# Cross-attention over 64 sequences: another order of loads in the first rounds, and two normalisings in the tail moved to ScalarE and GpSimd

## The chip, the core and the metric

The kernel runs on one core of a Trainium2 chip. The metric is the device time of one execution in microseconds; of several runs the median is given. The engines of the core are named as the profile names them: PE (TensorE, with PEld for its weight loads), DVE (VectorE), ACT (ScalarE), POOL (GpSimd) and SP (SyncE, which only issues DMAs here).

## What is computed

`x` is 64 x 256 x 512, `ctx` is 64 x 256 x 384, all in float32. Each of the 64 sequences goes through one cross-attention layer of hidden size 512:

```python
text_p  = einsum('bld,dh->blh', x,   W_text)  + b_text
audio_p = einsum('bsd,dh->bsh', ctx, W_audio) + b_audio
Q = layer_norm(text_p, g1, beta1)
K = layer_norm(audio_p, g2, beta2)
V = audio_p
alpha = softmax(einsum('blh,bsh->bls', Q, K) / sqrt(512), axis=-1)
H = einsum('bls,bsh->blh', alpha, V)
H = einsum('blh,hk->blk', H, W_out) + b_out
out = layer_norm(H + x, g_out, beta_out)
```

`layer_norm` takes mean and variance over the last axis, with an epsilon of 1e-5.

## The kernel before

**Staging.** The work is software-pipelined over rounds, one per sequence b, in an order written out by hand (each engine runs its instructions in the order in which the program names them). In round b the kernel computes the scores and the softmax of sequence b (`at`), the projection to Q and to K of sequence b+2 (`q2`, `k2`), the context product and output product of sequence b-1 (`last`), and the residual, the final layer norm and the store of sequence b-2 (`done`). Rounds run for b = 0 to 61; before them stands a start-up for sequences 0 and 1 and the folding of the weights, and behind them a written-out tail for sequences 62 (`at`) and 63 (`end`), in which `last` and `done` are sequences 61 and 60.

**Products.** The projections and the output product use a block scheme with seven products instead of eight (`Blocks.products` on PE, `Blocks.leave` for the evictions on DVE, line 483); each takes sums of blocks that POOL prepares (`sum_x`, `sum_c`). Their PSUM tiles are the pool `p_pj` of six banks; a bank is free again when both of its products have left. The scores are on line 511, the context product `ps_z` on line 577. W_audio and W_out are folded into one matrix at the start.

**Turning.** PE needs its operands with the contracted axis on the partitions. Outside the tail, the turning goes through DRAM and DVE: normalised Q and K rows and the exponentials are stored to DRAM (`qd`, `kd`, `ed`) and read back by four DMAs each, in squares (`squares`, line 88: `qq`, `kq`, `eq`), and DVE transposes 32x32 blocks (`turn`, line 91, and line 439). `x` and `ctx` are read the same way straight from the inputs (`xq`, `cq`; `load_x`, `load_c`) and turned by `turn_next(b + 3)`, which also makes the sums on POOL. The row-wise copies of `x` (for the residual, `add_x` on POOL, line 593) and of `ctx` (for the context product) are loaded by `load_rows` into pools of three buffers each.

**The DMA queue.** All these DMAs are issued by SP in program order, and an issue waits until its source is written. In a round of before the order is: `qq` and `kq` of b+1 (four each), `ed` of b, `cq` and `xq` of b+4 (four each), `eq` of b (four), the rows of x and of ctx of b+1, the output of b-2, `qd` and `kd` of b+2. `go_sb` and `beo_sb`, the scale and the shift of the last layer norm broadcast over the partitions, are loaded by two DMAs ahead of round 0.

**DVE in a round.** The order in a round from round 1 on: the last evictions of `done`, the turning of the exponentials of b-1 (`last.turn_e`, tile `eT`), of x and ctx of b+3 (`xT`, `cT`), the maxima of the scores (`nmx`), the evictions of `q2`, `q[b+1].turn`, the two `shift`s of `done`, `k[b+1].turn`, the two `settle`s of `done`, the evictions of `k2` and of `last`'s output. In round 0 `k[1].turn` and `turn_next(3)` stand at other places.

**The tail's last layer norms.** For each of the row tiles 0 and 1 of sequences 62 and 63: `evict` (line 632: PSUM times 1/denominator plus x, then mean and variance; `evict_halves` for the last one, lines 672 to 681), `scales` (POOL: variance plus epsilon, line 341; power of -0.5, line 343; the tiles `ve` and `rstd`), `shift` (DVE, line 698: minus the mean, times `go`), `settle` (DVE, line 703: times `rstd`, plus `beo`; `settle_halves`, line 686, for the last one), and the store.

Of the kernel before, what the change touches and what calls it, by code (L numbers as in the profile page):

```python
# [9 lines left out]
F32 = mybir.dt.float32  # L10
AF = mybir.ActivationFunctionType
ALU = mybir.AluOpType
# [3 lines left out]
P = 128  # L16
SQ = 32
NQ = P // SQ
EPS = 1e-05
# [3 lines left out]
def kernel(  # L23
# [41 lines left out]
    nc = tc.nc  # L65
    ctx.enter_context(tc.manual_schedule())
    B, L, D = x.shape
    S, DA = c.shape[1:]
    H = w_text.shape[1]
    LT, ST = L // P, S // P  # L70
    DC, AC, HC = D // P, DA // P, H // P
    scale = 1.0 / math.sqrt(H)

    const = ctx.enter_context(tc.tile_pool(name="const", bufs=1))
    xin = ctx.enter_context(tc.tile_pool(name="xin", bufs=3))
    cin = ctx.enter_context(tc.tile_pool(name="cin", bufs=3))
    blk = ctx.enter_context(tc.tile_pool(name="blk", bufs=2))
    work = ctx.enter_context(tc.tile_pool(name="work", bufs=2))
    small = ctx.enter_context(tc.tile_pool(name="small", bufs=4))
# [16 lines left out]
    def load_c(b):  # L96
        cq = blk.tile([P, S // SQ, DA // NQ], F32, tag="cq", name=f"cq_{b}")
        squares(cq, c[b])
        blocks[b] = [cq]

    def load_x(b):
        xq = blk.tile([P, L // SQ, D // NQ], F32, tag="xq", name=f"xq_{b}")
        squares(xq, x[b])
        blocks[b].append(xq)

    def load_squares(b):
        load_c(b)
        load_x(b)

    def load_rows(b):  # L110
        x_sb = xin.tile([P, LT, D], F32, tag="x", name=f"x_{b}")
        c_sb = cin.tile([P, ST, DA], F32, tag="c", name=f"c_{b}")
        nc.sync.dma_start(x_sb, x[b].rearrange("(t p) d -> p t d", p=P))
        nc.sync.dma_start(c_sb, c[b].rearrange("(t p) d -> p t d", p=P))
        return x_sb, c_sb

    ident = const.tile([P, P], F32, tag="ident", name="ident")
    make_identity(nc, ident)
    nhalf = const.tile([P, 2], F32, tag="nhalf", name="nhalf")
# [12 lines left out]
    def row(v, name):  # L132
        t = const.tile([P, H], F32, tag=name, name=name)
        nc.sync.dma_start(t, v.rearrange("(o h) -> o h", o=1).broadcast_to([P, H]))
        return t
# [4 lines left out]

    x_0 = xin.tile([P, LT, D], F32, tag="x", name="x_0")
    c_0 = cin.tile([P, ST, DA], F32, tag="c", name="c_0")
    c_rows, x_rows = [v[0].rearrange("(t p) d -> p t d", p=P) for v in (c, x)]
    wa_sb = const.tile([P, AC, H], F32, tag="wa", name="wa")
    wt_sb = const.tile([P, DC, H], F32, tag="wt", name="wt")

# [2 lines left out]
        for q in range(NQ):  # L149
            queues[q].dma_start(t[q * SQ : (q + 1) * SQ, lo : lo + n], v[q, :, lo : lo + n])  # L150

    nc.sync.dma_start(c_0[:, :1], c_rows[:, :1])
    weight_chunks(wa_sb, w_audio, 0, 1, [nc.scalar, nc.sync, nc.scalar, nc.sync])
    weight_chunks(wa_sb, w_audio, 1, 2, [nc.sync] * NQ)
    nc.sync.dma_start(c_0[:, 1:], c_rows[:, 1:])
    for t in range(LT):
        nc.sync.dma_start(x_0[:, t, :], x_rows[:, t, :])
    weight_chunks(wt_sb, w_text, 0, 2, [nc.sync] * NQ)
    ba_sb = row(b_audio, "ba")
    weight_chunks(wt_sb, w_text, 2, 2, [nc.sync] * NQ)  # L160
# [123 lines left out]
    H2 = H // 2  # L284
# [50 lines left out]
    def rstd_of(var, n, total=False):  # L335

        ve = small.tile([P, n], F32, tag="ve", name="ve")
        if total:
            nc.gpsimd.tensor_scalar(ve, var, 1.0 / D, EPS, ALU.mult, ALU.add)
        else:  # L340
            nc.gpsimd.tensor_scalar(ve, var, EPS, None, ALU.add)  # L341
        r = small.tile([P, n], F32, tag="rstd", name="rstd")
        nc.gpsimd.tensor_tensor(r, ve, nhalf[:, :n], ALU.pow)  # L343
        return [r[:, t : t + 1] for t in range(n)]
# [154 lines left out]
    class Attention:  # L499
        def __init__(self, b):  # L500
            self.b, self.qT, self.kT = b, q.pop(b).T, k.pop(b).T
            self.xb, self.c_sb = rows[b]

        def scores(self, end=False):
            if end:
# [84 lines left out]

        def add_x(self):
            for t in range(LT):
                nc.gpsimd.tensor_tensor(self.y[:, t, :], self.y[:, t, :], self.xb[:, t, :], ALU.add)  # L593

        def statistics(self):

# [34 lines left out]
        def evict(self, t):  # L631
            nc.vector.scalar_tensor_tensor(  # L632
                self.y[:, t, :],
                self.ps_y.pop(t),
                self.rden[:, t : t + 1],
                self.xb[:, t, :],
                ALU.mult,
                ALU.add,
            )
            moments(self.mv, self.y[:, t, :], t)  # L640

        def scales(self, lo=0, n=LT):
            self.r = getattr(self, "r", {})
            self.r.update({lo + t: r for t, r in enumerate(rstd_of(self.mv[:, lo : lo + n, 1], n))})

        def moments(self, tiles=range(LT)):
            if 0 in tiles:
# [20 lines left out]
        def evict_halves(self, t):  # L668
            st = small.tile([P, 2, 6], F32, tag="st2", name="st2")
            for h in range(2):  # L670
                half = self.y[:, t, bass.ts(h, H2)]
                nc.vector.scalar_tensor_tensor(
                    half,
                    self.ps_h[h],
                    self.rden[:, t : t + 1],
                    self.xb[:, t, bass.ts(h, H2)],
                    ALU.mult,
                    ALU.add,
                )
                nc.vector.bn_stats(st[:, h, :], half)  # L680
            nc.vector.bn_aggr(self.mv[:, t, :], st)
# [46 lines left out]
    def turn_next(b):  # L728
        xT[b] = turn_x(b)
        xs[b] = sum_x(xT.pop(b))  # L730
        cT[b] = turn_c(b)
        cs[b] = sum_c(cT.pop(b))

    def add_bias(b):
        xb = rows[b][0]
        for t in range(LT):
            nc.gpsimd.tensor_tensor(xb[:, t, :], xb[:, t, :], bao_sb, ALU.add)

    assert B > 3
    q, k, xT, cT, rows = {}, {}, {}, {}, {0: (x_0, c_0)}  # L740


    c_turn = RowTurn(c_0, AC, "cT")
# [105 lines left out]
    q[1].normalise()  # L849
    q[1].store()  # L850
    q[1].fetch()
    go_sb = row(g_out, "go")
    beo_sb = row(beta_out, "beo")

    done = last = None
    for b in range(B - 2):
        three = b + 3 < B
        at = Attention(b)
        at.scores()
        if done:  # L860
            done.o.leave(3)
            done.o.leave(7)
            done.o.leave(4)
            done.add_x()
        if last:
            last.turn_e()
        if three and b:
            turn_next(b + 3)
        at.maxima()
        at.exponentials()  # L870
        if not b:
            k[1].turn()
        q2 = q[b + 2] = Blocks("q", b + 2, xs.pop(b + 2), wt_blocks, bt_sb)
        q2.products(1, 2)
        q2.leave(1)
        at.reciprocals()
        at.divide_e()
        if not b:
            k[1].affine(g2_sb, be2_sb)
        if b:  # L880
            q[b + 1].fetch()
            k[b + 1].fetch()
        at.store_e()
        if b + 4 < B:
            load_squares(b + 4)
        at.fetch_e()
        rows[b + 1] = load_rows(b + 1)
        if done:
            done.statistics()
        q2.products(6, 5)  # L890
        q2.leave(6)
        q2.leave(2)
        q2.leave(5)
        q2.products(7, 3)
        q2.leave(3)
        q2.leave(7)
        q2.products(4)
        q2.leave(4)
        q2.square()
        q2.scales()  # L900
        q[b + 1].turn()
        if not b:
            turn_next(3)
        if done:
            done.shift(0)
            done.shift(1)
        if last:
            last.context()
        q[b + 1].affine(g1_sb, be1_sb)
        if b:  # L910
            k[b + 1].turn()
            k[b + 1].affine(g2_sb, be2_sb)
        if done:
            done.settle(0)
            done.settle(1)
            done.store()
        q2.normalise()
        q2.store()
        if last:
            last.start_products()  # L920
        k2 = k[b + 2] = Blocks("k", b + 2, cs.pop(b + 2), wa_blocks, ba_sb)
        k2.products(1, 2)
        k2.leave(1)
        k2.products(6, 5)
        k2.leave(6)
        k2.leave(2)
        k2.leave(5)
        k2.products(7, 3)
        k2.leave(3)
        k2.leave(7)  # L930
        k2.products(4)
        k2.leave(4)
        k2.square()
        k2.scales()
        k2.normalise()
        k2.store()
        if last:
            last.o.products(1, 2)
            last.o.leave(1)
            last.o.products(6, 5)  # L940
            last.o.leave(6)
            last.o.leave(2)
            last.o.leave(5)
            last.o.products(7, 3)
            last.o.products(4)
        done, last = last, at


    at = Attention(B - 2)
    q[B - 1].fetch()  # L950
    k[B - 1].fetch()
    rows[B - 1] = load_rows(B - 1)
    at.scores()
    done.o.leave(3)
    done.o.leave(7)
# [53 lines left out]
    at.multiply(1)  # L1009
    at.shift(0)  # L1010
    at.evict(1)
    at.scales(1, 1)
    at.settle(0)
    end.context()
    end.start_output()
    end.multiply(0)
    at.shift(1)
    at.settle(1)
    at.store()
    end.evict(0)  # L1020
    end.scales(0, 1)
    end.multiply_halves(1)
    end.shift(0)
    end.evict_halves(1)
    end.scales(1, 1)
    end.shift(1)
    end.settle(0)
    end.store(0, 1)
    end.settle_halves(1)

# [31 lines left out]
```

## Time and profile before

| | us |
|---|---|
| median of 3 runs | 1419.27 |
| lowest, highest of the runs | 1417.74, 1419.90 |
| the profiled execution | 1418.87 |
| its span in the profile | 1417.1 |
| mean time of a 128x256 scores matmul | 0.379 |
| shift or settle of a 128x512 row tile in the tail, DVE | 0.74 to 0.75 |
| addition on a 128x512 row tile, POOL (line 593) | 1.278 |
| ACT scaling a 128x512 row tile: scale alone; scale and bias | 0.714; 0.806 |
| `rstd` of one row tile, POOL | 0.56 to 0.93 |

The profile is of one execution; its span runs from the first to the last record, and the execution's time has 1.8 us more. "Busy" of an engine leaves out DMA issues and waits. Timelines give the start in us from the start of the span, the length, engine, line, operation, output and inputs, and in square brackets how long the engine was idle before and what ended that. The page puts 96% of the chain of work that ended last on PE.

### The profile page before, as it was taken

How to read it: one execution, taken by the hardware profiler on the slowest of the kernel's cores; microseconds unless marked ns; L12 is line 12 of the kernel's file. 1: busy time of each engine (PE TensorE's matmuls, PEld its weight loads, DVE VectorE, ACT ScalarE, POOL GpSimd, SP SyncE). 2: the span in 40 equal slices, each digit the busy share in tenths (PEclk: the TensorE clock that was granted, in tenths of full speed). 3: DMA queues.
4: the chain of work that ended last, by engine and by line, in shares of the span. 5: the costliest groups of instructions: out<-in, count | busy, mean ns of one | idle time of the engine just before them, and what ended most of it. 6: DMA issues, size and time to landing. Idle time of an engine off the chain costs nothing.

```text
span 1417.1 us, 23332 instructions
## 1 busy us (share of the span) xinstructions
PE 1404.4 (99%) x6441; PEld 1220.4 (86%) x6441; DVE 1273.0 (90%) x2134; ACT 931.8 (66%) x2293; POOL 878.0 (62%) x1295
## 2 busy tenths in 40 slices
PE   9999999999999999999999999999999999999997
PEld 5888888888888888888888888888888888888885
DVE  5789999999998999999999999999999999999988
ACT  4666676676676676765766766767667667667662
POOL 4556656666666666575566666665765666666645
PEclk9999999999999999999999999999999999999999
DMA  8898887888887788888878878887888788788763
GB/s 203 227 244 238 240 243 214 238 240 221 235 234 232 227 224 244 237 223 235 243 216 238 240 216 239 231 235 228 228 239 239 220 238 240 218 238 233 220 191 118
DMA packets 450583, 322.61 MB, mean 228 GB/s; under 512 B 154901, under 2 KB 382997, under 8 KB 450453
## 3 DMA queue, kind: packets, MB, share of 16 engines
q1 hardware_dynamic: 450356, 320.98, 79.9%
q8 instruction: 53, 0.87, 0.3%
q14 instruction: 78, 0.63, 0.2%
q10 hardware_dynamic: 96, 0.13, 0.0%
HBM read 204.09 MB, written 116.92 MB: 227 GB/s over the span
## 4 chain that ended last, share of the span: by engine, by line
PE 96%; DMA 1%; POOL 1%; DVE 1%; SPq 0%; issue 0%; ACT 0%; POOLq 0%; DVEq 0%; ACTq 0%
PE ps_q L472 27%; PE ps_y L472 21%; PE ps_k L472 21%; PE ps_sc L511 16%; PE ps_z L577 11%; DMA wt<-in_L_xattn_W_text_dram 1%; DMA xq<-in_x_dram 1%; POOL rstd L343 0%; PE ps_wao L245 0%; DVE st L267 0%; SPq L150 0%; POOL ve L341 0%; DVE y L632 0%; DVE y L698 0%; POOL wtsum L293 0%
## 5 line engine op out<-in xcount | busy, mean ns | idle before, releaser
L341 POOL TENSOR_SCALAR ve<-var 128x2 f32<-128x2 f32 x126 | 44.5, 353 | 305.9 <-ACT junk L380 305.9
L511 PE MATMUL ps_sc<-kT,qT 128*128 128x256 f32 x1024 | 231.5, 379 | 0.0
L528 ACT ACTIVATE e<-ps_sc,nmx 128x256 f32<-128x256 f32 x128 | 59.5, 469 | 246.4 <-DVE nmx L521 246.4
L483 DVE TENSOR_TENSOR qr<-ps_q,qr 128x512 f32<-128x512 f32 x378 | 188.0, 511 | 35.7 <-PE ps_q L472 24.0
L511 PEld LDWEIGHTS ps_sc<-kT,qT 128*128 128x128 f32 x1024 | 194.6, 190 | 26.9 <-ACT qT L446 0.2
L483 DVE TENSOR_TENSOR kr<-ps_k,kr 128x512 f32<-128x512 f32 x378 | 188.1, 511 | 24.3 <-PE ps_y L472 0.5
L483 DVE TENSOR_TENSOR yr<-ps_y,yr 128x512 f32<-128x512 f32 x372 | 185.1, 511 | 23.4
L593 POOL TENSOR_TENSOR yr<-yr,x 128x512 f32<-128x512 f32 x124 | 157.2, 1278 | 57.1 <-DVE yr L483 57.0
L577 PE MATMUL ps_z<-eT,c 128*128 128x256 f32 x768 | 176.5, 379 | 0.1
L472 PE MATMUL ps_q<-wtsum,xsum 128*128 128x256 f32 x756 | 173.6, 379 | 0.6 <-POOL xsum L305 0.6
L343 POOL TENSOR_TENSOR rstd<-ve,nhalf 128x2 f32<-128x2 f32 (+1 forms) x194 | 159.3, 821 | 16.2
L472 PE MATMUL ps_k<-wa,cT 128*128 128x256 f32 x630 | 166.8, 379 | 0.0
L472 PE MATMUL ps_y<-wao,zT 128*128 128x256 f32 x620 | 164.2, 379 | 0.0
L577 PEld LDWEIGHTS ps_z<-eT,c 128*128 128x128 f32 x768 | 145.8, 190 | 20.7 <-ACT e L528 0.5
L472 PEld LDWEIGHTS ps_q<-wtsum,xsum 128*128 128x128 f32 x756 | 143.6, 190 | 20.5 <-POOL xsum L305 1.0
L380 ACT ACTIVATE junk<-kr 128x512 f32<-128x512 f32 x126 | 79.3, 630 | 98.9 <-DVE kr L483 98.9
L446 ACT ACTIVATE qT<-qT,columns 128x256 f32<-128x256 f32 x256 | 132.8, 592 | 6.6 <-DVE qT L91 6.6
L472 PEld LDWEIGHTS ps_k<-wa,cT 128*128 128x128 f32 x630 | 119.6, 190 | 16.2
L446 ACT ACTIVATE kT<-kT,columns 128x256 f32<-128x256 f32 x256 | 132.1, 588 | 1.1 <-DVE kT L91 1.0
L472 PEld LDWEIGHTS ps_y<-wao,zT 128*128 128x128 f32 x620 | 117.7, 190 | 16.0
L408 ACT ACTIVATE kr<-kr,rstd 128x512 f32<-128x512 f32 x126 | 84.1, 714 | 70.7 <-POOL rstd L343 70.7
L703 DVE SCALAR_TENSOR_TENSOR yr<-yr,rstd,beo 128x512 f32<-128x512 f32 x124 | 127.5, 1066 | 0.6 <-POOL rstd L343 0.6
(150 smaller groups left out, 2945.9 us busy)
## 6 DMA issues: line engine op xcount, KB each, us to landing
kd<-kr SPq DMA_DIRECT2D x64, 512.0 KB, 3.1
kq<-kd SPq DMA_DIRECT2D x256, 128.0 KB, 3.4
qd<-qr SPq DMA_DIRECT2D x64, 512.0 KB, 5.5
qq<-qd SPq DMA_DIRECT2D x256, 128.0 KB, 3.3
xq<-in_x_dram SPq DMA_DIRECT2D x252, 128.0 KB, 2.9
x<-in_x_dram SPq DMA_DIRECT2D x63, 512.0 KB, 4.1
out_dram<-yr SPq DMA_DIRECT2D x62, 512.0 KB, 5.0
cq<-in_ctx_dram SPq DMA_DIRECT2D x252, 96.0 KB, 2.5
```

Source lines behind the costliest of these rows:

```text
L341: nc.gpsimd.tensor_scalar(ve, var, EPS, None, ALU.add)
L343: nc.gpsimd.tensor_tensor(r, ve, nhalf[:, :n], ALU.pow)
L380: nc.scalar.activation(junk, self.rows[:, t, :], AF.Square, scale=1.0 / math.sqrt(H), accum_out=self.var[:, t : t + 1],)
L408: nc.scalar.mul(row, row, self.r[t])
L446: nc.scalar.activation(self.T[:, k, :], self.T[:, k, :], AF.Identity, bias=bet[:, k : k + 1], scale=gam[:, k : k + 1],)
L472: nc.tensor.matmul(bank[:, j, :], lhsT=side, rhs=w, start=(i == 0), stop=(i == len(pairs) - 1))
L483: add = lambda o, i0, i1: nc.vector.tensor_tensor(o, i0, i1, ALU.add)
L511: nc.tensor.matmul(self.sc[:, t, :], lhsT=self.qT[:, k, bass.ts(t, P)], rhs=self.kT[:, k, :], start=(k == 0), stop=(k == HC - 1),)
L528: nc.scalar.activation(self.e[:, t, :], self.sc[:, t, :], AF.Exp, bias=self.nmx[:, t : t + 1], accum_out=self.den[:, t : t + 1],)
L577: nc.tensor.matmul(ps[:, j, :], lhsT=self.c_sb[:, s, bass.ts(lo + j, P)], rhs=self.eT[:, s, :], start=(s == 0), stop=(s == ST - 1),)
L593: nc.gpsimd.tensor_tensor(self.y[:, t, :], self.y[:, t, :], self.xb[:, t, :], ALU.add)
L703: nc.vector.scalar_tensor_tensor(self.y[:, t, :], self.y[:, t, :], self.r[t], beo_sb, ALU.mult, ALU.add)
```

## The change

In the rounds:

- The rows of x and of ctx are loaded by two functions, and the rows of x of sequence b in round b instead of round b-1 (round 61 loads those of 61 and 62; those of sequence 63 and all rows of ctx stay where they were).
- In round 0, `eq` is read ahead of `xq` instead of behind it.
- `go_sb` and `beo_sb` are loaded at the end of round 0, behind `kd` of sequence 2.
- From round 1 to 60, DVE turns x and ctx of b+3 before the exponentials of b-1.

In the tail:

- `scale_soon` puts the addition of epsilon on DVE and leaves the power on POOL, for row 1 of sequence 62 and both rows of 63.
- Row 1 of sequence 62 is settled by ACT (times `rstd`) and POOL (plus `beo`).
- Row 0 of sequence 63 is normalised by ACT (times `rstd`, minus mean times `rstd`) and POOL (times `go`, plus `beo`), in place of `shift` and `settle` on DVE.

The order of PE's instructions is the same. The diff, without renamings:

```diff
-    def load_rows(b):
-        x_sb = xin.tile([P, LT, D], F32, tag="x", name=f"x_{b}")
-        c_sb = cin.tile([P, ST, DA], F32, tag="c", name=f"c_{b}")
-        nc.sync.dma_start(x_sb, x[b].rearrange("(t p) d -> p t d", p=P))
-        nc.sync.dma_start(c_sb, c[b].rearrange("(t p) d -> p t d", p=P))
-        return x_sb, c_sb
+    def load_x_rows(b):
+        x_rows[b] = xin.tile([P, LT, D], F32, tag="x", name=f"x_{b}")
+        nc.sync.dma_start(x_rows[b], x[b].rearrange("(t p) d -> p t d", p=P))
+
+    def load_c_rows(b):
+        c_rows[b] = cin.tile([P, ST, DA], F32, tag="c", name=f"c_{b}")
+        nc.sync.dma_start(c_rows[b], c[b].rearrange("(t p) d -> p t d", p=P))
...
+        def scale_soon(self, t, shift=False):
+
+            r = small.tile([P, 1], F32, tag="rone", name="rone")
+            ve = small.tile([P, 1], F32, tag="veone", name="veone")
+            nc.vector.tensor_scalar(ve, self.mv[:, t, 1:2], EPS, None, ALU.add)
+            nc.gpsimd.tensor_tensor(r, ve, nhalf[:, :1], ALU.pow)
+            self.r = getattr(self, "r", {})
+            self.r[t] = r
+            if shift:
+                self.nmr = small.tile([P, 1], F32, tag="nmrone", name="nmrone")
+                nc.gpsimd.tensor_scalar(
+                    self.nmr, self.mv[:, t, 0:1], r, -1.0, ALU.mult, ALU.mult
+                )
+
+        def settle_beside(self, t):
+
+            row = self.y[:, t, :]
+            nc.scalar.mul(row, row, self.r[t])
+            nc.gpsimd.tensor_tensor(row, row, beo_sb, ALU.add)
+
+        def finish_beside(self, t):
+
+            row = self.y[:, t, :]
+            nc.scalar.activation(row, row, AF.Identity, bias=self.nmr, scale=self.r[t])
+            nc.gpsimd.tensor_tensor(row, row, go_sb, ALU.mult)
+            nc.gpsimd.tensor_tensor(row, row, beo_sb, ALU.add)
...
     q[1].fetch()
-    go_sb = row(g_out, "go")
-    beo_sb = row(beta_out, "beo")
...
             done.add_x()
+        if three and b:
+            turn_next(b + 3)
         if last:
             last.turn_e()
-        if three and b:
-            turn_next(b + 3)
         at.maxima()
...
         at.store_e()
         if b + 4 < B:
-            load_squares(b + 4)
-        at.fetch_e()
-        rows[b + 1] = load_rows(b + 1)
+            load_c(b + 4)
+        if not b:
+            at.fetch_e()
+        if b + 4 < B:
+            load_x(b + 4)
+        if b:
+            at.fetch_e()
+            load_x_rows(b)
+        if not three:
+            load_x_rows(b + 1)
+        load_c_rows(b + 1)
...
+        if not b:
+            go_sb = row(g_out, "go")
+            beo_sb = row(beta_out, "beo")
         done, last = last, at
...
     at.evict(1)
-    at.scales(1, 1)
+    at.scale_soon(1)
     at.settle(0)
     end.context()
     end.start_output()
     end.multiply(0)
     at.shift(1)
-    at.settle(1)
+    at.settle_beside(1)
     at.store()
     end.evict(0)
-    end.scales(0, 1)
+    end.scale_soon(0, shift=True)
     end.multiply_halves(1)
-    end.shift(0)
+    end.finish_beside(0)
     end.evict_halves(1)
-    end.scales(1, 1)
+    end.scale_soon(1)
     end.shift(1)
-    end.settle(0)
     end.store(0, 1)
     end.settle_halves(1)
```

More of the change, by code (lines that the diff above doesn't have):

```diff
@@ L142 @@
     c_0 = cin.tile([P, ST, DA], F32, tag="c", name="c_0")
-    c_rows, x_rows = [v[0].rearrange("(t p) d -> p t d", p=P) for v in (c, x)]
+    c_first, x_first = [v[0].rearrange("(t p) d -> p t d", p=P) for v in (c, x)]
+    x_rows, c_rows = {0: x_0}, {0: c_0}
     wa_sb = const.tile([P, AC, H], F32, tag="wa", name="wa")
@@ L150, in weight_chunks @@
             queues[q].dma_start(t[q * SQ : (q + 1) * SQ, lo : lo + n], v[q, :, lo : lo + n])
-    nc.sync.dma_start(c_0[:, :1], c_rows[:, :1])
+    nc.sync.dma_start(c_0[:, :1], c_first[:, :1])
     weight_chunks(wa_sb, w_audio, 0, 1, [nc.scalar, nc.sync, nc.scalar, nc.sync])
     weight_chunks(wa_sb, w_audio, 1, 2, [nc.sync] * NQ)
-    nc.sync.dma_start(c_0[:, 1:], c_rows[:, 1:])
+    nc.sync.dma_start(c_0[:, 1:], c_first[:, 1:])
     for t in range(LT):
-        nc.sync.dma_start(x_0[:, t, :], x_rows[:, t, :])
+        nc.sync.dma_start(x_0[:, t, :], x_first[:, t, :])
     weight_chunks(wt_sb, w_text, 0, 2, [nc.sync] * NQ)
@@ L501, in __init__ @@
             self.b, self.qT, self.kT = b, q.pop(b).T, k.pop(b).T
-            self.xb, self.c_sb = rows[b]
+            self.c_sb = c_rows[b]
         def scores(self, end=False):
@@ L592, in add_x @@
             for t in range(LT):
-                nc.gpsimd.tensor_tensor(self.y[:, t, :], self.y[:, t, :], self.xb[:, t, :], ALU.add)
+                nc.gpsimd.tensor_tensor(self.y[:, t, :], self.y[:, t, :], x_rows[self.b][:, t, :], ALU.add)
         def statistics(self):
@@ L635, in evict @@
                 self.rden[:, t : t + 1],
-                self.xb[:, t, :],
+                x_rows[self.b][:, t, :],
                 ALU.mult,
@@ L675, in evict_halves @@
                     self.rden[:, t : t + 1],
-                    self.xb[:, t, bass.ts(h, H2)],
+                    x_rows[self.b][:, t, bass.ts(h, H2)],
                     ALU.mult,
@@ L734, in add_bias @@
     def add_bias(b):
-        xb = rows[b][0]
+        xb = x_rows[b]
         for t in range(LT):
@@ L739 @@
     assert B > 3
-    q, k, xT, cT, rows = {}, {}, {}, {}, {0: (x_0, c_0)}
+    q, k, xT, cT = {}, {}, {}, {}
     c_turn = RowTurn(c_0, AC, "cT")
@@ L951 @@
     k[B - 1].fetch()
-    rows[B - 1] = load_rows(B - 1)
+    load_x_rows(B - 1)
+    load_c_rows(B - 1)
     at.scores()
```

## The prediction

> **What bounds the kernel now.** I read the page's busy times first, then the windows view over the four stretches that the timeline suggested, then the timelines of one engine at a time where TensorE has a gap. First line: the page. The others: stretch, its length, then busy time and instructions of PE, PEld, DVE, ACT, POOL, the granted clock, the DMA share and GB/s.
>
> ```profile
> PE 1404.4 (99%) x6441; PEld 1220.4 (86%) x6441; DVE 1273.0 (90%) x2134; ACT 931.8 (66%) x2293; POOL 878.0 (62%) x1295
> ...
> 36.90:79.50 42.60, 42.54 (x186) 35.26 (x186) 32.92 (x52) 26.23 (x61) 24.89 (x43) 1.00 0.90 231
> 79.50:80.90 1.40, 0.05 (x2) 0.07 (x1) 1.30 (x3) 1.40 (x5) 0.00 (x0) 1.00 1.07 231
> 80.90:1381.70 1300.80, 1300.80 (x6027) 1145.13 (x6028) 1188.59 (x1989) 877.75 (x2169) 814.38 (x1197) 1.00 0.81 231
> 1381.70:1417.10 35.40, 27.59 (x113) 19.97 (x111) 28.66 (x52) 10.00 (x24) 19.71 (x23) 0.96 0.39 118
> ```
>
> From 80.9 to 1381.7 TensorE has no idle time, so nothing that the change does to a steady round can shorten it; it can only lengthen it. What can be won is one gap of 1.35 us in round 1 and part of the last 35 us. The diff touches nothing before 54 us.
>
> The gap, first in the timelines of DVE and PE (start, length, engine, line, operation, the idle time before it and what ended it), then SyncE's queue ahead of it:
>
> ```profile
> 66.46 0.71 DVE L91 STREAM_TRANSPOSE eT<-eq 128x512 f32<-128x512 f32 x1 [2.73 <-DMA eq<-ed]
> ...
> 77.58 1.30 DVE L439 STREAM_TRANSPOSE kT<-kq 128x512 f32<-128x512 f32 x2 [0.94 <-DMA kq<-kd]
> ...
> 80.86 0.67 PE L472 MATMUL ps_y<-waosum,zsum 128*128 128x256 f32 x2 [1.35 <-DVE kr L483]
> ```
>
> ```profile
> 54.09 0.45 SPq L134 DMA_DIRECT2D go<-in_L_xattn_g_out_dram  x1
> ...
> 57.69 4.60 SPq L88 DMA_DIRECT2D xq<-in_x_dram  x4
> 62.42 1.85 SPq L88 DMA_DIRECT2D eq<-ed  x4
> ...
> 66.98 0.37 SPq L418 DMA_DIRECT2D kd<-kr  x1
> 71.15 1.80 SPq L88 DMA_DIRECT2D qq<-qd  x4
> 73.05 1.88 SPq L88 DMA_DIRECT2D kq<-kd  x4
> ```
>
> TensorE stops because a PSUM bank of `ps_k` is not yet evicted. DVE is late with it because `k[2].turn` stands ahead of the evictions and starts at 77.58, when `kq` lands. The 2.73 us wait for `eq` is the larger number, but it is not last: DVE waits again for `qq` (1.23) and `kq` (0.94) after it.
>
> The end, in the timelines of DVE and POOL:
>
> ```profile
> 1407.20 0.74 DVE L632 SCALAR_TENSOR_TENSOR y<-ps_y,rden,x 128x512 f32<-128x512 f32 x1
> ...
> 1412.57 0.93 POOL L343 TENSOR_TENSOR rstd<-ve,nhalf 128x1 f32<-128x1 f32 x1
> ...
> 1413.54 0.88 DVE L686 SCALAR_TENSOR_TENSOR y<-y,rstd,beo 128x256 f32<-128x256 f32 x2 [0.46 <-POOL rstd L343]
> ```
>
> DVE carries the end from 1399 on; its last step waits for the last `rstd` of GpSimd.
>
> **Part 1, the first two rounds.** Now `ed(0)` no longer queues behind `go` and `beo`, and is issued at 54.09 instead of 55.11. `eq` needs it landed: `ed` lands after the `qq` ahead of it, whose data DVE had at 56.55. In round 1 `ed` was issued 0.1 us after `kq`, as here after `qq`, and was landed by 79.50, 4.5 us later; so at most 58.6 here. Then `eq` (1.9 us of issue), `xq` (1.9 to 2.0), landing 2.65 after the last issue, as `kq` did (74.93 to 77.58): `xq` lands at 64 to 65. DVE's new order is xT 1.20, cT 0.94, eT 0.70, overlapping by 0.1: eT is done by 67 to 68, and `ps_z` needs it at 69.41. Cover 1.5 to 2.4 us. If `ed` took the 6.5 us that it took behind the biases, eT would come at about 69.9: cost +0.5. `qd(2)` goes at about 62.2 instead of 65.39, as `x(1)` and two bias loads are out of its way.
>
> What sets the gap is `kq(2)`, and its source `kd` cannot be issued before 66.98, because it follows ScalarE's normalising of `kr` (ends 66.96), which nothing in the change moves. Behind `kd` the queue now holds `go` and `beo`: 67.4 and 67.9. Before, the second and third issue of `xq` waited 1.1 and 0.7 us for these two, each standing eight issues behind one of them (transfers take eight completion signals in turn, so an issue waits for the eighth before it); that puts their landings at 59.2 and 60.4, 5.1 and 5.8 us after issue. In the new order the third and fourth issue of `kq` stand eight behind `go` and `beo`. They go at about 72.6 and 73.7; the last ends at 74.1, and lands 2.65 later: 76.8. The other bound is bytes: kd, go, beo, qq, kq are 2.1 MB, at the 231 GB/s of this stretch 9.1 us from 67.0, so 76.1 with no lag and 78.7 with the 2.65. I take 77.0, near the first, since it rests on the same transfers. The gap closes when `kq` lands by 77.58 − 1.35 = 76.23; at 77.0 it keeps 0.8. **Term: −0.6 us (−1.35 to +1.1, and +0.5 more if eT is late).**
>
> **Part 2, steady rounds.** DVE turns x and ctx before e, so eT starts 2.0 us later in each round: in the round whose eT stands at 711.44 it would end at 714.1 instead of 712.1, and `ps_z` begins at 718.50. Cover 4.4 us; `nmx` behind the three keeps its time. xsum on POOL, which waited 0.54 us per round for xT, starts earlier; it is needed a round later. `x(b)` instead of `x(b+1)` in round b is the same 512 KB; it is read by `add_x` two rounds later, and no longer waits for POOL (5.0 us in 27 waits, behind none of which TensorE stood idle). The last round loads two, when the four-part loads have ended. **Term: 0; it would cost 3 us if each of 61 rounds lost 0.05, which needs a cover of 4.4 us to go.**
>
> **Part 3, the tail.** The instruction order is the same on PE; ScalarE gains two passes, DVE loses a settle, a shift and a settle (L703, L698: 0.75 each) and gets three tiny additions for `ve`, taken at 0.13 to 0.15 (L538's reciprocal). GpSimd loses three `ve` of 0.63 to 0.78 and gains three adds and multiplies on 128x512, a `nmr`, and keeps its order, which is the point. Step by step:
> - `at`'s row 1: shift ends at 1406.2 instead of 1406.06, ScalarE multiplies 0.71 (L408), GpSimd adds beo 1.28 (L593, same shape) and is free at 1408.4.
> - `end`'s row 0: evict no longer waits for DVE (1407.20) but for TensorE, which ends at 1406.81: starts 1406.85. Then 0.75, statistics 0.71, 0.19, `ve` 0.15: 1408.7.
> - GpSimd pow 0.57, nmr 0.27, ScalarE with scale and bias 0.81 (L410), GpSimd times go 1.28, plus beo 1.28, with six hand-overs of 0.05 to 0.08: 1413.3.
> - Only then comes the last pow, of row 1, as it stands behind these in GpSimd's order, though its `ve` is ready at 1410.8: 0.57, so the last settle starts at 1413.95 instead of 1413.54.
>
> Row: pow takes 0.93 when DVE runs a step on two SBUF inputs beside it (1405.57, 1412.57) and 0.56 to 0.57 otherwise; here DVE is idle by then. Bounds: all at their shortest (adds 1.25) +0.1; both pows 0.93, nmr 0.6 like the slowed `ve`, adds 1.47 (L593 in the tail, 2.94 for two) +1.9. I take +0.4, the sum of the undisturbed rows. **Term: +0.4 us (+0.1 to +1.9).**
>
> The Trainium skill, GPSIMD Engine Reference, section Engine selection, speaks against this part: elementwise work of two inputs belongs on VectorE, GpSimd being about twice as slow. This trace has 1.28 against 0.74, 1.7 times; by the page's factor the two adds on the path would take an estimated 2.96 instead of 2.56, and the term would be +0.8.
>
> **Sum.** −0.6 + 0 + 0.4 = −0.2 us on the profiled execution of 1418.87 (span 1417.1 and 1.77 around it), which is 0.40 below the median 1419.27: 1418.7. A measurement of this kernel tells about 0.2%, 2.8 us, from no change; this is well inside.
>
> **Rivals.**
> - *The gap stays as it is*: the `eq` wait goes, `kq` still lands at 77.6, as the biases take the place of `x(1)` in the queue. For: the bytes. Start 0, tail +0.4: 1419.3. Chance 0.25.
> - *Faster*: `kq` lands by 76.2 and the last pow isn't held. Then shift(1) ends at 1411.5 and the settle follows: −2.0 in the tail, −1.35 in the gap, 1415.5. Against: GpSimd's order holds the pow behind 2.56 us of work that itself starts after ScalarE. Chance 0.10.
> - *Slower*: `go` and `beo`, now between `kd` and the reads that TensorE waits for, hold `kq` back for long. For: while they ran, at 56 to 58, the DMA engines were 0.92 to 0.98 busy and moved 117 and 150 GB/s. Each us after 76.23 costs one; with the tail at +0.4 it passes 0.2% when `kq` lands after 80.0. At 80.5: gap 4.3, +2.9, with the tail 1422.2. Against: 78.7 is my bytes-and-lag bound. Chance 0.13.
> - The forecast itself: 0.52.
>
> **Numbers.** Within 0.2%: 0.52 + 0.25 = 0.77; faster 0.10; slower 0.13. Low end: −1.25 (gap closed, tail at its best) and 0.8 of the spread of the runs (1417.74 to 1419.90): 1416.8. High end: +1.1 in the gap and +1.5 in the tail, 1421.4.
>
> **What would show it.** Right: in round 1 DVE no longer waits for `eq`, but still for `kq`, at about 77; the gap on PE at 79.5 is under 1.35; rounds stay at 21.58 us; the last `rstd` on POOL starts right behind an add with beo, near 1413.3 less what the gap gave. Wrong: a new PE wait for eT near 69.4 or in steady rounds; `kq` landing after 79; the last `rstd` starting near 1411.

## The result: 0.25% slower, and where the time went

The changed kernel took 1423.03 us (median of 22 runs, 1420.47 to 1424.75), the kernel before 1419.08 in the same series. The ratio is 1.0025, with a 95% interval of 1.0018 to 1.0031. The forecast was 1418.7, no difference, with a range up to 1421.4. The profiled execution took 1424.13, its span is 1422.3.

Cut at the first and the last scores matmul, the two spans compare like this:

| us | before | changed | difference |
|---|---|---|---|
| start of the span to the first scores | 45.67 | 45.03 | -0.64 |
| first scores to the end of the last | 1350.24 | 1355.54 | +5.30 |
| from there to the end of the span | 21.19 | 21.73 | +0.54 |

Nothing that runs before the first scores was moved (the bias loads stood ahead of them in the program, but were issued at 54.09), and other profiles of this study have 45.05 to 46.56 there, so the first row is the spread between executions. The third row is the tail; spans are given to 0.1 us, so tails are good to 0.05. The second is the loss. The profiled execution is one of the slower of the 22: the medians differ by 3.95 us, the two profiled executions by 5.26.

The page's busy line of the changed kernel, then its windows view in five stretches (columns as before):

```profile
PE 1407.6 (99%) x6441; PEld 1223.4 (86%) x6441; DVE 1271.0 (89%) x2134; ACT 933.6 (66%) x2295; POOL 873.6 (61%) x1296
```

```profile
36.00:78.00 42.00, 42.00 (x185) 34.86 (x184) 31.27 (x51) 23.82 (x56) 24.64 (x43) 1.00 0.85 208
78.00:82.00 4.00, 0.86 (x5) 0.41 (x3) 2.93 (x5) 3.39 (x7) 0.00 (x0) 0.96 1.09 251
82.00:92.00 10.00, 9.37 (x30) 7.83 (x31) 9.10 (x17) 4.65 (x10) 5.47 (x7) 0.68 0.82 257
92.00:1386.35 1294.35, 1294.35 (x5999) 1139.61 (x5998) 1179.23 (x1975) 874.00 (x2160) 803.27 (x1191) 1.00 0.81 231
1386.35:1422.30 35.95, 27.61 (x113) 19.98 (x111) 27.90 (x52) 11.53 (x26) 21.57 (x24) 0.92 0.38 116
```

Two things are to be seen. From 92 to 1386 TensorE is as full as it was: the new order in the 60 steady rounds costs nothing. And all that was lost lies between 78 and 92, in two columns: TensorE is idle, and then, while it is busy again, its granted clock is 0.68 on average. PE's busy time grew by 3.2 us with the same 6441 matmuls.

The chain of waits in this place, in order of time (start, length, what), first before, then changed:

```profile
80.86 2.40 PE ps_y L472 x10
83.25 3.45 PE ps_sc L511 x16
```

```profile
67.55 7.20 DMA beo<-in_L_xattn_beta_out_dram
...
74.77 4.46 DMA kq<-kd
...
82.63 4.61 PE ps_y L474 x10
87.23 4.14 PE ps_sc L513 x16
```

SyncE's queue ahead of it, and the timelines of DVE and of PE:

```profile
66.62 0.37 SPq L420 DMA_DIRECT2D kd<-kr  x1
67.04 0.46 SPq L135 DMA_DIRECT2D go<-in_L_xattn_g_out_dram  x1
67.55 0.83 SPq L135 DMA_DIRECT2D beo<-in_L_xattn_beta_out_dram  x1
68.48 2.08 SPq L88 DMA_DIRECT2D qq<-qd  x4
70.61 4.46 SPq L88 DMA_DIRECT2D kq<-kd  x4
```

```profile
65.77 0.67 DVE L91 STREAM_TRANSPOSE eT<-eq 128x512 f32<-128x512 f32 x1
...
77.14 1.25 DVE L91 STREAM_TRANSPOSE qT<-qq 128x1024 f32<-128x1024 f32 x1 [5.70 <-DMA qq<-qd]
79.35 1.30 DVE L441 STREAM_TRANSPOSE kT<-kq 128x512 f32<-128x512 f32 x2 [0.97 <-DMA kq<-kd]
```

```profile
82.63 1.19 PE L474 MATMUL ps_y<-waosum,zsum 128*128 128x256 f32 x2 [3.76 <-DVE kr L485]
```

The wait of DVE for `eq` is gone, as meant. But `qq`, issued by 70.56, is there only at 77.1, and DVE stands 5.70 us. `kq` follows, DVE reaches the evictions of `ps_k` later than before, and the gap on PE is 3.76 us instead of 1.35: +2.41. Behind it ten matmul steps of `ps_y` take 4.61 us, where before they took 2.40, and the scores 4.14 instead of 3.45: +2.90. Together 5.31, which is the second row of the table.

In 5 of the 22 runs the mean granted clock was 0.999, and these took 1420.47 to 1421.60; in the other 17 it was 0.995 to 0.998, and they took 1422.45 to 1424.75. So the halved clock is probably not in every run. That is not shown: only one run has a trace, and 0.998 also occurs in runs of the kernel before, whose clock falls only at the end of its profile.

### The profile page after: what moved, and what is told of

The parts are those of the page before. It is cut to its first block, busy times and chain, and to the rows that moved or that the text cites. A ratio compares the mean times of both kernels' runs of the same rounds, so it can differ in the third digit from the quotient of the medians.

```text
span 1422.3 us, 23460 instructions
## 1 busy us (share of the span) xinstructions
PE 1407.6 (99%) x6441; PEld 1223.4 (86%) x6441; DVE 1271.0 (89%) x2134; ACT 933.6 (66%) x2295; POOL 873.6 (61%) x1296
## 4 chain that ended last, share of the span: by engine, by line
PE 97%; DMA 1%; DVE 0%; ACT 0%; POOL 0%; issue 0%; POOLq 0%; SPq 0%; DVEq 0%
PE ps_q L474 26%; PE ps_k L474 21%; PE ps_y L474 21%; PE ps_sc L513 16%; PE ps_z L579 11%; PE ps_wao L247 1%; PE ps_y L625 1%; DMA beo<-in_L_xattn_beta_out_dram 1%; PE ps_q L364 1%; PE ps_k L364 0%; DMA kq<-kd 0%; PE ps_ones L195 0%; DVE kr L485 0%; PE ps_rows L211 0%; POOLq L1096 0%
## 5 line engine op out<-in xcount | busy, mean ns | idle before, releaser
L345 POOL TENSOR_TENSOR rstd<-ve,nhalf 128x2 f32<-128x2 f32 x191 | 156.9, 822 | 15.9
```

## The experiments

Each is told by its difference to the kernel before or to the changed kernel. The ratios are to the kernel before, run beside it. The table cuts the profiles as above.

| us | first to last scores | tail | ratio, 95% interval |
|---|---|---|---|
| before | 1350.24 | 21.19 | |
| changed | 1355.54 | 21.73 | 1.0025 [1.0018, 1.0031] |
| bias loads early again | 1350.42 | 21.73 | 1.0000 [0.9992, 1.0009] |
| bias loads alone moved | 1353.64 | 21.18 | 1.0021 [1.0012, 1.0030] |
| changed, bias loads in round 1 | 1348.65 | 21.80 | 0.9991 [0.9983, 1.0000] |
| tail alone changed | 1350.45 | 21.80 | 1.0003 [0.9994, 1.0012] |
| plain loads in their place | 1349.49 | 21.99 | 0.9993 [0.9984, 1.0002] |
| gap filled with work | 1352.22 | 21.75 | 1.0014 [1.0005, 1.0023] |
| split tail | 1348.84 | 20.86 | 0.9980 [0.9971, 0.9989] |
| last power ahead | 1348.85 | 22.29 | 0.9991 [0.9982, 0.9999] |
| bias loads in round 1, old tail | 1348.72 | 21.17 | 0.9978 [0.9968, 0.9988] |
| before, bias loads in round 1 | 1349.00 | 21.18 | 0.9976 [0.9967, 0.9986] |

### Which part of the change costs

**The bias loads early again.** Edit, on the changed kernel:

```diff
     q[1].fetch()
+    go_sb = row(g_out, "go")
+    beo_sb = row(beta_out, "beo")
...
-        if not b:
-            go_sb = row(g_out, "go")
-            beo_sb = row(beta_out, "beo")
```

> The changed kernel with the loads of go and beo back ahead of round 0; all else as changed. Theory (the two bias loads behind kd hold back the reads of q and k in round 1, TensorE idles 3.8 us at 78.9 and then runs at a granted clock of 0.5 for 7 us): kq lands before 77.6, the gap is between 0 and 1.35 us, no stretch of halved clock, and with the tail's +0.55 us the time is 0.8 us under to 0.6 us over the kernel before (ratio 0.9994 to 1.0004). Rival (turning x and ctx before e, or the shifted x rows, cost the time): still 3 to 4 us over the kernel before (ratio 1.0025).

Within the range of the theory: the loss is gone with the move undone. The gap of 1.5 us that is left is another one than before, by the waits view of PE:

```profile
PE ps_z L579 <- DVE eT L91: 1.5, 1, 1.5
```

With the biases ahead of `ed`, `eq` goes at 61.2, `xq` behind it lands at 67.7, and DVE, which now turns x first, brings eT late. This is the case that the prediction priced at 0.5; it costs 1.5.

**The bias loads alone moved.** On the kernel before, the two lines of the change and nothing else.

> The kernel before with nothing but the loads of go and beo moved to the end of round 0. Theory: x of sequence 1 is still loaded in round 0, so kq lands at least as late as in the changed kernel (79 to 81), the gap is 3.5 to 5 us, the clock halves behind it in most runs: 3 to 6 us over the kernel before (ratio 1.002 to 1.004). Rival (the order of turning or the tail costs the time): no different from the kernel before within 0.05%.

As the theory had it: `qq` makes DVE wait 6.24 us, PE stands still for 3.34, and the clock is 0.50 from 82.3 to 85.7. The timelines of DVE and of PE:

```profile
77.48 1.25 DVE L91 STREAM_TRANSPOSE qT<-qq 128x1024 f32<-128x1024 f32 x1 [6.24 <-DMA qq<-qd]
82.86 1.19 PE L472 MATMUL ps_y<-waosum,zsum 128*128 128x256 f32 x2 [3.34 <-DVE kr L483]
```

By the ratios, this one edit of the change makes nearly its whole loss. Its profile has 3.40 us of the 5.30 between the scores: the gap is a little narrower, and the clock is at half for 3.4 us instead of 6.8.

**The tail alone.** On the kernel before, the tail of the change and its three functions.

> The kernel before with nothing but the tail of the change. Theory: the last pow starts behind GpSimd's multiplication and addition for row 0; from the end of the last scores to the end of the span 21.7 us instead of 21.2: 0.5 us over the kernel before (ratio 1.0004), gap of round 1 as before. Rival (the tail is the cost of the change): 3 us over.

The timed ratio can't tell 0.0004 from nothing, but the tail in the profile is 21.80 against 21.19, and the other profiles with one tail or the other agree to 0.1 us, but for the one with plain loads (21.99). The new tail costs 0.5 to 0.6.

### What is slow about the bias loads, and why the gap costs double

**Plain loads in their place.** On the kernel of the next section, whose bias loads in round 1 then fill the same two tiles, at the end of round 0:

```diff
+        if not b:
+            go_sb = const.tile([P, H], F32, tag="go", name="go")
+            beo_sb = const.tile([P, H], F32, tag="beo", name="beo")
+            nc.sync.dma_start(go_sb, x[9][:P])
+            nc.sync.dma_start(beo_sb, x[9][P:])
```

> The kernel with the bias loads in round 1, plus, at the end of round 0 where the change has the bias loads, two loads of 256 KB each from 128 different rows of x into the same two tiles (which the bias loads fill later). Theory A (it is the bytes): kq lands as late as in the changed kernel, 79, and PE idles 3 to 4 us. Theory B (it is that all 128 partitions read one row of 2 KB; go and beo moved at 100 to 150 GB/s): the plain loads pass in 2.3 us at 231 GB/s, kq lands at 75 to 77, and the gap is 0 to 0.8 us: time within 1 us of the kernel with the bias loads in round 1.

It is theory B. DVE starts on `kq` at 76.41 instead of 79.35, and the gap is 0.5 us. The timeline of DVE with plain loads:

```profile
74.36 1.25 DVE L91 STREAM_TRANSPOSE qT<-qq 128x1024 f32<-128x1024 f32 x1 [2.79 <-DMA qq<-qd]
76.41 1.30 DVE L441 STREAM_TRANSPOSE kT<-kq 128x512 f32<-128x512 f32 x2 [0.81 <-DMA kq<-kd]
```

The windows view by single microseconds shows the difference (the last two columns are DMA share and GB/s, of all DMAs together); first the changed kernel, then the plain loads:

```profile
69.00:70.00 1.00, 1.00 (x6) 0.90 (x5) 0.90 (x3) 0.20 (x1) 1.00 (x3) 1.00 0.72 137
70.00:71.00 1.00, 1.00 (x7) 0.87 (x6) 0.88 (x2) 0.72 (x2) 0.16 (x1) 1.00 0.91 102
71.00:72.00 1.00, 1.00 (x6) 0.88 (x5) 0.42 (x1) 0.53 (x1) 0.00 (x0) 1.00 1.18 154
72.00:73.00 1.00, 1.00 (x6) 0.89 (x5) 0.00 (x0) 0.94 (x4) 0.64 (x2) 1.00 0.89 153
```

```profile
69.00:70.00 1.00, 1.00 (x7) 0.87 (x6) 0.87 (x3) 0.33 (x1) 1.00 (x3) 1.00 0.99 283
70.00:71.00 1.00, 1.00 (x6) 0.87 (x5) 0.97 (x2) 0.65 (x2) 0.21 (x1) 1.00 1.06 368
71.00:72.00 1.00, 1.00 (x6) 0.90 (x5) 0.47 (x2) 0.47 (x2) 0.00 (x0) 1.00 1.20 210
```

In both traces the two loads are 256 packets of 2 KB, the first of them at about 69.0. The last ends at 74.0 in the changed kernel and at 71.2 with plain loads, where the row of 210 GB/s is already the reading of `qq`. So the same 512 KB with the same shape of destination take 2.2 us when each partition reads a row of its own, and 5.0 when all 128 read one row. Busy DMA engines alone don't explain it: with the gap filled (the next experiment), the loads end as late, at 74.2, though the engines are only 0.25 busy in this microsecond:

```profile
71.00:72.00 1.00, 1.00 (x7) 0.87 (x6) 0.77 (x2) 0.47 (x3) 0.00 (x0) 1.00 0.25 82
```

Why one row is slow was not looked into.

**The gap filled.** On the changed kernel, ahead of the products that wait:

```diff
+            if b == 1:
+                ps = p_at.tile([P, P], F32, tag="at", name="ps_ones")
+                for _ in range(16):
+                    nc.tensor.matmul(ps, lhsT=ones, rhs=ones, start=True, stop=True)
             last.o.products(7, 3)
```

> The changed kernel with 16 extra multiplications of the constant ones on TensorE in round 1, ahead of the output products that wait (their result is not used). Theory (the idle time of 3.8 us is what halves the granted clock behind it): the gap stays as wide, filled with the extra work, no stretch at 0.5, and 3.1 us less than in those runs of the changed kernel that were throttled: 1.5 to 2.3 us over the kernel before (ratio 1.0011 to 1.0016) in all runs. Rival (the clock falls for another reason, the gap being only where it shows): stretch of 0.5 as before, ratio 1.0025.

The timeline of PE shows the extra work in the gap (each of the 16 is recorded as two), and the next product behind it at its usual pace (0.60 for two steps, against 1.19 in the changed kernel):

```profile
79.30 3.73 PE L982 MATMUL ps_ones<-ones 128*128 128x128 f32 x32
82.88 0.60 PE L474 MATMUL ps_y<-waosum,zsum 128*128 128x256 f32 x2
```

`kq` is as late as in the changed kernel (DVE starts on it at 79.30), but the granted clock stays at 1.00, and the stretch between the scores is 3.3 us shorter: the 2.90 of the slowed matmuls and a little more. In time the ratios are 1.0014 and 1.0025, with intervals that overlap; 10 of its 11 runs are under 1422.6, one took 1424.2. That the idle time brings the low clock rests on the profiles.

### Versions that keep what was good

**Bias loads in round 1.** On the changed kernel:

```diff
         load_c_rows(b + 1)
+        if b == 1:
+            go_sb = row(g_out, "go")
+            beo_sb = row(beta_out, "beo")
```

> The changed kernel with the loads of go and beo in round 1, behind the rows of ctx, instead of at the end of round 0. Theory: nothing stands between kd and the reads of q and k in round 1; kq lands by 75, the gap of round 1 is gone, and no new gap comes in round 2: start -1.35, tail +0.55, so 0.8 us under the kernel before (ratio 0.9994). If the bias loads only carry the delay with them, a gap of 1 to 4 us stands in round 2 instead. Rival (order of turning, x rows): 3 to 4 us over the kernel before.

The ratio was expected at 0.9994 and measured at 0.9991. There is no gap any more in any round, as DVE starts on `kq` at 74.38, by its timeline:

```profile
74.38 1.30 DVE L441 STREAM_TRANSPOSE kT<-kq 128x512 f32<-128x512 f32 x2 [1.14 <-DMA kq<-kd]
```

**The same move on the kernel before.** Only the two bias loads, put behind the rows of ctx of round 1.

> The kernel before with nothing but the loads of go and beo moved into round 1, behind the rows of ctx. Theory (the bias loads alone make the gap of the kernel before, too, as ed and eq stand behind them): no wait for eq, kq lands by 76.2, gap 0 to 0.3 us, ratio 0.9990 to 0.9993. Rival (the order of eq and xq and the rows of x are needed for it): gap of 1 us or more remains, ratio 0.9998 to 1.

DVE starts on `kq` at 75.76, PE has no gap: 1.2 us less between the scores, with none of the other edits. Ahead of round 0 the bias loads had been the cause of the old gap, too. The measured ratio, 0.9976, is lower than the profile's 1.2 us would give, and the kernel before ran at 1420.08 in that series instead of 1418.8 to 1419.5; the part that the spans show is safe, the rest may be spread. The runs of the kernel before reach from 1418.73 to 1422.83 there, those of this version from 1416.98 to 1418.83; no slow run of the kernel before has a trace, so what makes it slow stays open.

**With the old tail.** The changed kernel with bias loads in round 1 and the tail of before.

> The kernel with the bias loads in round 1, with the tail of the kernel before. Theory (the new tail costs 0.4 to 0.6 us): ratio to the kernel before 0.9989 to 0.9991, and from the end of the last scores to the end of the span 21.2 us instead of 21.7. Rival (the new tail costs nothing, or gains): the same as with the new tail, or slower.

The tail is 21.17 again. The ratio is lower than expected, in the same series as the last one and with the same reserve.

**The last power ahead.** With bias loads in round 1:

```diff
-    end.finish_beside(0)
     end.evict_halves(1)
     end.scale_soon(1)
+    end.finish_beside(0)
```

> The kernel with the bias loads in round 1, and in the tail the last power ahead of GpSimd's multiplication and addition for row 0. Theory: the halves of row 1 are settled 2 us earlier and the store of row 0 becomes the last, issued 0.9 us earlier than the last store was: ratio 0.9985. Rival (the 256 KB of row 0 take longer to land than the 128 KB halves): the gain is 0.2 us or nothing.

A miss: the tail grew from 21.80 to 22.29. The power did come ahead of GpSimd's passes, but DVE's last two steps, 0.88 together in the changed kernel, took 2.88 beside these. First DVE's timeline, then POOL's:

```profile
1411.46 2.88 DVE L715 SCALAR_TENSOR_TENSOR y<-y,rone,beo 128x256 f32<-128x256 f32 x2 [0.44 <-POOL rone L653]
```

```profile
1411.40 1.25 POOL L672 TENSOR_TENSOR y<-y,go 128x512 f32<-128x512 f32 x1
1412.73 1.32 POOL L673 TENSOR_TENSOR y<-y,beo 128x512 f32<-128x512 f32 x1
```

The first half ended at 1412.94 and the second at 1414.34, each 0.3 us after a pass of GpSimd. The Trainium skill, SBUF — State Buffer, section Who interferes with whom, says that a VectorE instruction with two inputs in SBUF contends with a GpSimd instruction that reads SBUF, and that the ports which the two share are an exclusive lock. The rows agree: each step ends only behind a pass, and takes 1.48 and 1.40 instead of the 0.48 and 0.40 that it needs alone.

**The split tail.** With bias loads in round 1, DVE adds `beo` to row 0, GpSimd only multiplies by `go`:

```diff
-    end.finish_beside(0)
+    row0 = end.y[:, 0, :]
+    nc.scalar.activation(row0, row0, AF.Identity, bias=end.nmr, scale=end.r[0])
+    nc.gpsimd.tensor_tensor(row0, row0, go_sb, ALU.mult)
...
     end.shift(1)
+    nc.vector.tensor_tensor(row0, row0, beo_sb, ALU.add)
     end.store(0, 1)
```

> The kernel with the bias loads in round 1, and in the tail the addition of beo to row 0 of the last sequence by DVE instead of GpSimd. Theory (GpSimd's order holds the last pow behind both of its passes over row 0): the pow starts 1.3 to 1.6 us earlier, DVE has an addition of 0.7 more; the last store goes 1.4 us earlier than with the bias loads in round 1 alone: ratio 0.9982 to 0.9984 to the kernel before. Rival (the tail is bound by the store of row 0 or by DVE): no more than 0.3 us.

Tail 20.86, 0.9 less than the changed tail and 0.3 less than the old one; the last store goes 1.1 us earlier, 1.4 was expected. The power stands behind one pass instead of two, and DVE settles right behind its own addition, without a wait (timelines of POOL and of DVE):

```profile
1410.82 1.00 POOL L653 TENSOR_TENSOR rone<-veone,nhalf 128x1 f32<-128x1 f32 x1
```

```profile
1411.93 0.87 DVE L715 SCALAR_TENSOR_TENSOR y<-y,rone,beo 128x256 f32<-128x256 f32 x2
```

Its median is 1416.95 us, the lowest of the study, with a ratio of 0.9980: it beats both kernels. The versions with the old tail are within what these runs can tell.

## Why the prediction was wrong

- **When `kq` lands (part 1).** This is the step that failed. 77.0 was forecast, with a bound of 78.7, and DVE started on it at 79.35; the gap grew by 2.41 us where the term had it shrink by 0.6. The two bias loads were counted as bytes at 231 GB/s, and by landings of 5.1 and 5.8 us after issue. They moved at 102 to 154 GB/s and, by SyncE's waits, landed after 5.9 and 7.2. The lines that said so (117 and 150 GB/s at 56 to 58) were used for a rival alone, not for the bound. The 2.65 us from the last issue of `kq` to its landing were too short as well: 4.3 here, and 4.2 with plain loads. What fits ordinary traffic is the sum by bytes, 76.1, against 76.41 with plain loads.
- **What held `kq` back.** The third and fourth issue of `kq` waited for `go` and `beo` as forecast (1.3 and 1.4 us), and the last one ended at 75.07 instead of 74.1; the profile's chain goes through it. But `qq`, issued in time, was late too, and `kq` came 2.2 us behind it, as before (2.18) and with plain loads (2.05), where no issue waited that long. Whether the late issues alone would have cost anything is not shown.
- **What a gap costs (part 1 and the slower rival).** "Each us after 76.23 costs one" left out a term, the slowed matmuls behind the gap: 2.90 us, more than the gap's own growth. The gap of 1.35 us before leaves the clock at 1.00, but the prediction's own row for the last stretch has 0.96: the clock falls at the end, 5.2 us after the last matmul. The Trainium skill, TensorE: Matmul & The Clock Gate, Part 1: The HAM clock gate, gives the rule that was not weighed: after about 3.4 us without work the clock is halved, and it returns after about as long at work; an estimate by it would have been up to 1.7 us for a stretch of 3.4 at half clock. Here the clock fell 2.8 us after the last matmul and stayed low for 6.8 us; with the bias loads alone moved, 2.8 and 3.4. Both stays are whole multiples of about 3.4. The idle time until the fall is not fixed: at the ends of the twelve profiles it is 2.2 to 5.2 us, so the page's 3.4 is no safe bound, and that gaps of 3.3 and 3.8 us met a fall was probably in part luck.
- **The rest of part 1** held: `qd(2)` went at 61.96 (forecast 62.2), eT was done at 66.4 (67 to 68), and PE did not wait for it.
- **Part 2** held: no idle time in steady rounds.
- **Part 3** held in kind, 0.4 forecast, 0.5 to 0.6 measured, at the place forecast. The timelines of POOL and DVE at the end:

```profile
1415.32 1.26 POOL L672 TENSOR_TENSOR y<-y,go 128x512 f32<-128x512 f32 x1 [0.93 <-ACT y L671]
1416.66 1.59 POOL L673 TENSOR_TENSOR y<-y,beo 128x512 f32<-128x512 f32 x1
1418.21 0.54 POOL L653 TENSOR_TENSOR rone<-veone,nhalf 128x1 f32<-128x1 f32 x1
```

```profile
1415.45 1.68 DVE L727 SCALAR_TENSOR_TENSOR y<-y,mvy,go 128x512 f32<-128x512 f32 x1
...
1418.79 0.88 DVE L715 SCALAR_TENSOR_TENSOR y<-y,rone,beo 128x256 f32<-128x256 f32 x2 [1.66 <-POOL rone L653]
```

  The last power starts right behind the addition of `beo`, and DVE waits 1.66 us for it. The sum was short in the addition, 1.59 instead of 1.28, beside a shift on DVE that itself took 1.68 instead of 0.75: they met.
- **The rivals.** It went the way of the third one, slower, at 0.13, and not as it was priced: about half of the loss between the scores is the gap, and half the clock. That rival named what held `kq` back, but took the loss to pass 0.2% only when `kq` lands after 80.0. The first, that the bias loads take the place of `x(1)` by their bytes, was not it: with as many bytes in plain loads `kq` came at 76.41.

## What to carry to other kernels

A transfer that nobody waits for still has a place in the queue: put it where the next reads that the bound engine needs are not right behind it, and price it by the rate at which transfers of its kind move in the trace, not by its bytes at the mean rate. Where TensorE is full, a gap is not worth its own length alone: in the profiled run, one that grew from 1.35 to 3.8 us cost a further 2.9 us at half clock. And work handed to another engine is late by what stands ahead of it in that engine's order, and slow by what it shares with the engine it came from.

## What the runs showed of the hardware

- Two loads of 256 KB in which 128 partitions read the same row of 2 KB landed 5.9 and 7.2 us after issue, and held the reads behind them for 2.8 to 2.9 us more than two plain loads of the same size.
- TensorE's granted clock went from 1.00 to 0.50 at 2.8 us of idle time in two gaps, and back after 6.8 and 3.4 us; with gaps of 1.35 to 1.6 us it stayed at 1.00. At the ends of the profiles, where no work follows, it fell 2.2 us (changed kernel) to 5.2 us (before) after the last matmul. Three single microseconds of the changed kernel that show the fall in the gap and the return, clock in the third column from the end:

```profile
81.00:82.00 1.00, 0.00 (x0) 0.00 (x0) 0.90 (x2) 1.00 (x3) 0.00 (x0) 0.83 1.14 219
85.00:86.00 1.00, 1.00 (x4) 0.82 (x3) 0.88 (x2) 0.35 (x2) 0.48 (x2) 0.50 1.03 389
88.00:89.00 1.00, 1.00 (x5) 0.86 (x4) 0.90 (x3) 0.00 (x0) 1.00 (x2) 0.76 0.29 111
```

- A DVE step on two SBUF inputs of 0.48 us took 1.48 beside a GpSimd pass over 128x512.
